# Cross-attention on one core: which engine's queue issues the first pair of block swaps

## The chip, the core and the metric

The kernel runs on one core of one Trainium2 chip. The metric is the device time of one execution in microseconds (us), the median of several runs. The engines are named as in the profile: PE is TensorE, DVE is VectorE, ACT is ScalarE, POOL is GpSimd and SP is SyncE, which only issues transfers here. "ACTq" and "SPq" are rows of an engine's instruction queue, such as the issue of a DMA transfer.

## What is computed

A layer norm, a query projection, attention of 32 heads of width 32 over a context of 256 rows, an output projection and a residual. The keys and the values are the context itself.

```python
mu, var = mean(x), var(x)                                    # x: (8, 256, 1024), float32
xn = (x - mu) * rsqrt(var + 1e-5) * ln_gamma + ln_beta
Q = split_heads(xn @ Wq.T)                                   # 32 heads of 32
K = V = split_heads(ctx)                                     # ctx: (8, 256, 1024)
scores = einsum('bhsd,bhtd->bhst', Q, K) * 32 ** -0.5        # masked where mask is False
attn = einsum('bhst,bhtd->bhsd', softmax(scores), V)
out = x + merge_heads(attn) @ Wout.T
```

## The kernel before

The order of all work is written out by hand (`manual_schedule`): each engine executes its instructions in the order in which the program lists them, and semaphores hold it where data or a buffer is not ready.

**Quads.** The work of attention is cut into N = 64 quads: eight batches, and in each eight groups of four heads (NQ = 8). One pass of the main loop (line 926) is about one quad deep on every engine. In the pass of quad n, TensorE makes the scores of quad n+1 (`scores`, L486), multiplies the probabilities of quad n-2 with the values (`values`, L629), and beside these it makes steps of the query projection of a later batch (L345, L447) and of the output projection of an earlier one (L715). The output projection and most of the query projection are Strassen-like sums of products: seven products in place of eight, whose results DVE adds out of PSUM (`take`, `store`; L753, L757) or ACT copies. The PSUM bank `po_S` or `po_A` is used again by the next product as soon as that sum has read it.

**The softmax of a quad** (`softmax_parts`) runs for n+1 during the pass of quad n. For each of four heads and two halves of 128 rows, DVE adds the mask and takes the row minimum (L522), ACT takes the exponential and its row sum (L526), DVE inverts the sums (L533, one for each head), POOL multiplies (L535, two for each head), and DVE transposes the head in 32x32 blocks (L541, `blocks`). So eight exponentials and four block transposes for each quad.

**The swaps.** After the four block transposes, half of the blocks of the tile `pT` lie on the wrong group of 32 partitions. To swap them, ACT first copies one half aside into `pc` (L547, `aside`, two copies for each quad), then two transfers of 128 KB overwrite this half with their partners (L607, the first pair, `pT<-pT`), and, after they have landed, two more bring the copies from `pc` to where the partners were (L611, the second pair, `pT<-pc`). The last block transpose, the second copy aside and the four transfers form the quad's `tail`. It runs at the end of the quad's softmax for quads 8 to 56 and for the last one, and inside the next softmax for the others. Two passes later `values` reads `pT`; `pT` has three buffers and `pc` two.

**The transfers.** All but two small ones at the start are issued by SP, in program order: for each quad the load of values (`ahead`, L144), the first pair, loads of keys, of x, of residual rows or of weights (`between`), the second pair, and in three quads of a batch also 4, 6 and 6 transfers of 64 KB that move the normalized x of a later batch between partitions (`move_x`, L332). Stores of results (L758) come from the sums in PSUM. Every transfer raises one of eight completion semaphores, given out in turn in program order; before an issue that reuses one, the issuing engine waits for the transfer that had it before.

In two quads of a batch, ACT also normalizes half of a later batch's x (`ln_norm`, L252), between the tail of one quad and the exponentials of the next.

Of the kernel before, what the change touches and what calls it, by code (L numbers as in the profile page):

```python
# [59 lines left out]
def xattn_kernel(  # L60
# [11 lines left out]
    nc = tc.nc  # L72
# [4 lines left out]
    NQ = NC  # L77
# [4 lines left out]
    K = 32  # L82
# [4 lines left out]
    N = B * NQ  # L87
# [405 lines left out]
            pass  # L493

    tails = []


    def softmax_parts(n, copies=(), ahead=(), between=(), hooks={}, fill=()):

        fill = list(fill)

        def fill_in():
            if fill:
                fill.pop(0)()

        pss = scs[n]  # L510
        pT = pTs[n] = ptp.tile([P, 2, NI, NH, NS, K], F32, tag="pT", name=f"pT_{n}")
        pc = asp.tile([P, NI, NH, NS, K], F32, tag="pc", name=f"pc_{n}")
        es, mns, dens = {}, {}, {}

        def exps(j, part=range(NS)):
            if 0 in part:
                es[j] = ep.tile([P, NS, T], F32, tag="e", name=f"e_{n}_{j}")
                mns[j] = sm.tile([P, NS], F32, tag="mn", name=f"mn_{n}_{j}")
                dens[j] = sm.tile([P, NS], F32, tag="den", name=f"den_{n}_{j}")
            e, mn, den = es[j], mns[j], dens[j]  # L520
            for s in part:
                nc.vector.tensor_tensor_reduce(  # L522
                    out=e[:, s, :], in0=pss[j][:, s, :], in1=mbs[n // NQ], scale=1.0,
                    scalar=NO_SCORE, op0=ALU.add, op1=ALU.min, accum_out=mn[:, s : s + 1],
                )
                nc.scalar.activation(  # L526
                    e[:, s, :], e[:, s, :], AF.Exp, bias=mn[:, s : s + 1], scale=-1.0,
                    accum_out=den[:, s : s + 1],
                )

        def normalize(j):
            rden = sm.tile([P, NS], F32, tag="rden", name=f"rden_{n}_{j}")
            nc.vector.reciprocal(rden, dens[j])  # L533
            for s in range(NS):
                nc.gpsimd.tensor_scalar(  # L535
                    es[j][:, s, :], es[j][:, s, :], rden[:, s : s + 1], 1.0,
                    ALU.mult, ALU.mult,
                )

        def blocks(j):  # L540
            nc.vector.transpose(  # L541
                pT[:, :, :, j, :, :].rearrange("p a i s k -> p (a i) s k"),
                es[j].rearrange("p s (b t) -> p b s t", t=K),
            )

        def aside(j):
            nc.scalar.copy(pc[:, :, ts(j, 2)], pT[:, 1, :, ts(j, 2)])  # L547

        if n == 0:
            for j in range(NH - 1):  # L550
                exps(j, (0,))
            yield
            exps(NH - 1, (0,))
            fill_in()
            yield
            for j in range(NH):
                exps(j, (1,))
            normalize(0)
            fill_in()
        else:  # L560
            exps(0)
            while tails:
                tails.pop()()
            late = "p1" in hooks
            if not late:
                for done in list(pvs):
                    copy_at(done)
            exps(1)
            for hook in hooks.get("soon", ()):
                hook()  # L570
            exps(2)
            normalize(0)
            for hook in hooks.get("p1", ()):
                hook()
            exps(3)
            if late:
                for done in list(pvs):
                    copy_at(done)
        if n <= NQ:
            for copy in copies:  # L580
                copy()
        for hook in hooks.get(0, ()):
            hook()
        normalize(1)
        fill_in()
        blocks(0)
        for hook in hooks.get(1, ()):
            hook()
        normalize(2)
        fill_in()  # L590
        blocks(1)
        aside(0)
        normalize(3)
        fill_in()
        blocks(2)
        while fill:
            fill_in()
        if n > NQ:
            for copy in copies:
                copy()  # L600

        def tail():
            blocks(3)
            aside(1)

            for r in range(2):
                nc.sync.dma_start(pT[ts(2 * r, K), 1], pT[ts(2 * r + 1, K), 0])  # L607
            for load in between:
                load()
            for r in range(2):  # L610
                nc.sync.dma_start(pT[ts(2 * r + 1, K), 0], pc[ts(2 * r, K)])  # L611

        for load in ahead:
            load()
        if n < NQ or N - NQ < n < N - 1:
            tails.append(tail)
        else:
            tail()
        yield
# [16 lines left out]
    def copy_at(n):  # L636
        b, c = divmod(n, NQ)
        k, c = divmod(c, NK)
        if c == 0:
            ats[b, k] = atp.tile([P, NK, NS, NA, K], F32, tag="at", name=f"at_{b}_{k}")  # L640
        for r, pv in enumerate(pvs.pop(n)):
            nc.scalar.copy(
                ats[b, k][:, c, :, ts(r, 2), :], pv.rearrange("p a s k -> p s a k")
            )
# [262 lines left out]
    for b in range(B - 1):  # L907
        done, ends = 0, b == B - 2
        for i, counts in enumerate(steps_of(b)):
            n = NQ * (b + 1) + i  # L910
# [227 lines left out]
```

## Time and profile before

| | |
|---|---|
| time, median of 3 runs | 577.23 us (576.55 to 578.54) |
| profiled execution, first to last instruction (span) | 577.0 us |
| PE busy | 567.3 us (98%) |
| DVE, ACT, POOL busy | 460.4, 411.7, 409.8 us |
| granted TensorE clock, mean | 0.997 |
| first-pair transfers issued by SP | 128, 3.1 us to landing (median) |

The span is the profiled execution's own time from its first to its last instruction, and no other time of that execution is given. The median of the runs is 0.23 us above it. A row of the timeline gives the start, the duration, engine, line and operation, and in brackets the idle time before it and what ended it. A row of the waits gives the engine and line that waited, for whom, the total in us, the number of times and the longest. Issues of transfers are not counted as busy time.

### The profile page before, as it was taken

Reading aid. Unit: us, or ns where it says so; the run is one execution under the profiler, and the core shown is the slowest. Engines: PE = TensorE matmul, PEld = TensorE weight load, DVE = VectorE, ACT = ScalarE, POOL = GpSimd, SP = SyncE. Lnnn points to the kernel's source line nnn. Section 1 sums busy time; section 2 is a strip of 40 time slices with the busy share of each in tenths; the row PEclk is TensorE's granted clock in tenths of the full one; section 3 lists DMA queues with packets and bytes.
Section 4 is the critical chain, followed back from the end, with each engine's and each line's share of the span. In section 5 each row is a group of like instructions: output and inputs, shape, how many; then the busy total and the mean of one; then the engine's idle time right before and its main releaser. Section 6 shows DMA issues by size and latency. Waiting matters only on the chain. (4 is left out here: it accounts for less than half of the span.)

```text
span 577.0 us, 20128 instructions
## 1 busy us (share of the span) xinstructions
PE 567.3 (98%) x7162; PEld 394.2 (68%) x7162; DVE 460.4 (80%) x1695; ACT 411.7 (71%) x1425; POOL 409.8 (71%) x677
## 2 busy tenths in 40 slices
PE   8999998999999999999999999999999999999997
PEld 8788784667667777677676677667766767755543
DVE  5888887788877879979888788988878878779823
ACT  4697886677667877688677867768767776769810
POOL 1778898889896896876568675676658657448770
PEclk9999999899999999999999999999999999999999
DMA  8974766656677777957678856687567864446751
GB/s 304 394 206 126 208 161 180 192 148 166 185 220 222 200 208 207 271 166 201 188 213 228 211 138 189 212 240 206 148 161 236 224 170 130 130 138 178 199 166 73
DMA packets 50100, 111.69 MB, mean 194 GB/s; under 512 B 9424, under 2 KB 10192, under 8 KB 50000
## 3 DMA queue, kind: packets, MB, share of 16 engines
q1 hardware_dynamic: 49712, 110.40, 66.8%
q8 instruction: 57, 0.93, 0.7%
q14 instruction: 43, 0.35, 0.2%
q10 hardware_dynamic: 288, 0.01, 0.0%
HBM read 60.04 MB, written 10.49 MB: 122 GB/s over the span
## 5 line engine op out<-in xcount | busy, mean ns | idle before, releaser
L535 POOL TENSOR_SCALAR e<-e,rden 128x256 f32<-128x256 f32 x512 | 236.0, 478 | 116.9 <-DVE rden L533 114.4
L526 ACT ACTIVATE e<-e,mn 128x256 f32<-128x256 f32 x512 | 253.9, 501 | 50.7 <-DVE mn L522 49.6
L541 DVE STREAM_TRANSPOSE pT<-e 128x512 f32<-128x512 f32 x256 | 180.9, 707 | 44.7 <-POOL e L535 32.7
L522 DVE CUSTOM_DVE_ANT_0 e<-sc,mb 128x256 f32<-128x256 f32 x512 | 185.4, 416 | 26.4 <-PE sc L486 26.0
L547 ACT COPY pc<-pT 128x512 f32<-128x512 f32 x128 | 79.0, 617 | 72.1 <-DVE pT L541 36.6
L526 ACT ACTIVATION_READ_ACCUMULATOR e<-e,mn 128x1 f32 x512 | 97.9, 191 | 0.0
L345 PE MATMUL pq<-xnT,wq 128*128 128x256 f32 (+1 forms) x368 | 84.1, 383 | 0.6 <-ACT qa L354 0.6
L345 PEld LDWEIGHTS pq<-xnT,wq 128*128 128x128 f32 x368 | 68.9, 190 | 15.4 <-issue 3.7
L629 PE MATMUL pv<-pT,v 64*32 64x128 f32 x4096 | 74.7, 274 | 3.5 <-DMA v<-in_kv_dram 2.9
L629 PEld LDWEIGHTS pv<-pT,v 64*32 64x32 f32 x4096 | 57.5, 105 | 26.7 <-issue 14.7
L486 PEld LDWEIGHTS sc<-k,qa 32*128 32x128 f32 x1024 | 46.2, 184 | 41.9 <-issue 23.6
L715 PE MATMUL po_S<-wo,at 128*128 128x512 f32 x152 | 74.3, 606 | 0.0
L486 PE MATMUL sc<-k,qa 32*128 32x256 f32 x1024 | 73.6, 401 | 0.1
L715 PE MATMUL po_A<-wo,at 128*128 128x512 f32 x128 | 61.2, 620 | 0.3 <-ACT qa L354 0.3
L715 PE MATMUL po_S<-wo,s 128*128 128x512 f32 x104 | 49.9, 606 | 0.0
L533 DVE RECIPROCAL rden<-den 128x2 f32<-128x2 f32 x256 | 37.6, 147 | 7.7 <-ACT e L526 6.8
L522 DVE DVE_READ_ACCUMULATOR2_ANT mn<- 128x1 f32 x512 | 42.5, 83 | 0.0
L715 PEld LDWEIGHTS po_A<-wo,at 128*128 128x128 f32 x128 | 23.4, 193 | 26.2 <-issue 24.5
L447 PEld LDWEIGHTS pq_A<-xnT,wq 128*128 128x128 f32 x320 | 37.3, 192 | 4.8 <-issue 3.6
L715 PEld LDWEIGHTS po_S<-wo,at 128*128 128x128 f32 x152 | 25.8, 190 | 19.7 <-issue 19.1
L447 PE MATMUL pq_A<-xnT,wq 128*128 128x128 f32 x320 | 37.3, 275 | 0.0
L748 POOL TENSOR_TENSOR r<-r,p 128x512 f32<-128x512 f32 x23 | 29.4, 1278 | 7.1 <-DMA r<-in_x_dram 3.3
(96 smaller groups left out, 608.7 us busy)
## 6 DMA issues: line engine op xcount, KB each, us to landing
v<-in_kv_dram SPq DMA_DIRECT2D x64, 256.0 KB, 3.9
pT<-pT SPq DMA_DIRECT2D x128, 128.0 KB, 3.1
pT<-pc SPq DMA_DIRECT2D x128, 128.0 KB, 3.5
ring<-kept_T SPq DMA_DIRECT2D x18, 512.0 KB, 5.2
k<-in_kv_dram SPq DMA_DIRECT2D x32, 256.0 KB, 3.1
x<-in_x_dram SPq DMA_DIRECT2D x14, 512.0 KB, 5.1
r<-in_x_dram SPq DMA_DIRECT2D x28, 256.0 KB, 5.1
out_dram<-r SPq DMA_DIRECT2D x28, 256.0 KB, 3.0
```

Source lines behind the costliest of these rows:

```text
L345: nc.tensor.matmul(pqs[n], wq[:, o, c, :], xnTs[b](c), start=(c == 0), stop=(c == NC - 1),)
L447: nc.tensor.matmul(pqs[b][:, o, :], w[:, c], x_[:, c], start=begins and o + c == 0, stop=c == NK - 1, skip_group_check=True,)
L486: nc.tensor.matmul(scs[n][j][:, s, :], qa[r, n % NQ, ts(s, P)], ks[n - n % 2][r, n % 2, :], start=True, stop=True,)
L522: nc.vector.tensor_tensor_reduce(out=e[:, s, :], in0=pss[j][:, s, :], in1=mbs[n // NQ], scale=1.0, scalar=NO_SCORE, op0=ALU.add, op1=ALU.m ...
L526: nc.scalar.activation(e[:, s, :], e[:, s, :], AF.Exp, bias=mn[:, s : s + 1], scale=-1.0, accum_out=den[:, s : s + 1],)
L533: nc.vector.reciprocal(rden, dens[j])
L535: nc.gpsimd.tensor_scalar(es[j][:, s, :], es[j][:, s, :], rden[:, s : s + 1], 1.0, ALU.mult, ALU.mult,)
L541: nc.vector.transpose(pT[:, :, :, j, :, :].rearrange("p a i s k -> p (a i) s k"), es[j].rearrange("p s (b t) -> p b s t", t=K),)
L547: nc.scalar.copy(pc[:, :, ts(j, 2)], pT[:, 1, :, ts(j, 2)])
L629: nc.tensor.matmul(pvs[n][r][j * HD : (j + 1) * HD], vs[n][ts(r, 2 * K), i, ts(j, HD)], pT[ts(r, 2 * K), :, i, j, :, :], start=(i == 0), s ...
L715: nc.tensor.matmul(po, operand(b, name)[:, c], wo[:, which, c], start=begins and c == 0, stop=c == NK - 1, skip_group_check=not begins,)
L748: nc.gpsimd.tensor_tensor(r, r, p1s[b], ALU.add)
```

## The change

For quads 10 to 56 the first pair of swaps is issued on ACT's queue, in program order right behind the quad's second copy aside, and no longer on SP's. The loads and the second pair stay on SP, in their order. 47 quads with two transfers each are 94 issues.

```diff
     tails = []
+    BY_ACT = range(NQ + 2, N - NQ + 1)
 ...
             blocks(3)
             aside(1)
 
+            queue = nc.scalar if n in BY_ACT else nc.sync
             for r in range(2):
-                nc.sync.dma_start(pT[ts(2 * r, K), 1], pT[ts(2 * r + 1, K), 0])
+                queue.dma_start(pT[ts(2 * r, K), 1], pT[ts(2 * r + 1, K), 0])
             for load in between:
                 load()
             for r in range(2):
                 nc.sync.dma_start(pT[ts(2 * r + 1, K), 0], pc[ts(2 * r, K)])
```

## The prediction

> **What bounds the kernel now.** I read the waits of PE and SP first, then the busy time of each engine batch by batch, then the timeline around the tails. Waits of PE, of ACT for DVE's minima, and of SP's queue:
>
> ```profile
> PE pv L629 <- DMA v<-in_kv_dram: 2.9, 2, 2.1
> PE pv L629 <- DMA pT<-pT: 0.5, 1, 0.5
> ACT e L526 <- DVE mn L522: 49.6, 48, 3.6
> SPq L611 <- DMA pT<-pT: 75.9, 59, 6.2
> ```
>
> SP waits long for the first pairs to land (75.9 us), but PE has waited for a swap once, for 0.5 us. Busy time of two batches, from scores to scores (the stretch and its length; busy PE, weight loads, DVE, ACT and POOL with their instructions; granted clock, busy share of the DMA engines, GB/s):
>
> ```profile
> 293.33:361.26 67.93, 67.93 (x922) 48.06 (x921) 58.21 (x213) 51.39 (x179) 45.95 (x80) 1.00 0.70 194
> 361.26:430.21 68.95, 68.10 (x921) 48.20 (x921) 58.47 (x212) 51.52 (x179) 45.99 (x80) 1.00 0.70 195
> ```
>
> In the first batch PE is busy for every one of the 67.93 us, at full clock; in the second, 0.85 us are missing. So PE sets the time, 67.93 / 8 = 8.49 us for a quad, and a change of issuing engine cannot shorten it by more than the waits that PE has inside quads 10 to 56. ACT, at 51.39 of 67.93 us, seems to have room, but it is in a loop with DVE and POOL, which has to be counted quad by quad.
>
> **What the change can save.** The 0.85 us are one late load of values:
>
> ```profile
> 357.06 1.15 SPq L607 DMA_DIRECT2D pT<-pT  x2
> 358.25 0.57 SPq L136 DMA_DIRECT2D k<-in_kv_dram  x1
> 358.87 0.43 SPq L130 DMA_DIRECT2D x<-in_x_dram  x1
> 360.45 1.15 SPq L611 DMA_DIRECT2D pT<-pc  x2
> 361.65 5.03 SPq L332 DMA_DIRECT2D xnT<-xe  x6
> 366.77 0.53 SPq L758 DMA_DIRECT2D out_dram<-r  x1
> 367.39 0.41 SPq L144 DMA_DIRECT2D v<-in_kv_dram  x1
> 367.89 1.15 SPq L607 DMA_DIRECT2D pT<-pT  x2
> ...
> 370.90 0.86 PE L629 MATMUL pv<-pT,v 64*32 64x128 f32 x36 [0.85 <-DMA v<-in_kv_dram]
> ```
>
> SP was late: it had spent 357.06 to 358.21 on quad 39's first pair, and after its loads it stood from 359.30 (358.87 + 0.43) to 360.45 for that pair's landing. With the pair on ACT, issued when the copy ends, both fall away, and the second pair, the six moves and the load of values come 1.15 + 1.15 = 2.3 us earlier. So this wait goes: -0.85 us. The other wait for values (2.9 - 0.85 = 2.05 us) is for quad 8, whose load and the swaps before it come ahead of quad 10; I leave it. No other PE wait in the range is for a transfer, so the swaps' own landing, sooner or later, is worth nothing.
>
> **What it adds on ACT.** The price of an issue on ACT at this size is not in the trace. The rows next to it are SP's issue of the same pair (quad 39's, above, and quad 46's behind its copy), and the two small issues of ACT beside four loads of SP at the start:
>
> ```profile
> 412.98 0.62 ACT L547 COPY pc<-pT 128x512 f32<-128x512 f32 x1 [1.50 <-DVE pT L541]
> 413.62 1.14 SPq L607 DMA_DIRECT2D pT<-pT  x2
> ...
> 0.72 0.41 ACTq L195 DMA_DIRECT2D gam<-in_gamma_dram  x1
> 1.16 0.45 ACTq L196 DMA_DIRECT2D bet<-in_beta_dram  x1
> 0.72 1.80 SPq L130 DMA_DIRECT2D x<-in_x_dram  x4
> ```
>
> SP issues 0.02 us after the copy's end (412.98 + 0.62 = 413.60), takes 1.15 us for the pair (357.06 to 358.21) and goes on 0.04 us later. At the start ACT's issues took 0.41 and 0.45 us where SP's took 0.45 on average (1.80 / 4), so I charge ACT what SP pays: C = 0.02 + 1.15 + 0.04 = 1.21 us from the end of a copy aside to ACT's next operation. The low end is two issues at 0.41 and 0.45, C = 0.96 with the gaps; the high end is one more SP issue of 0.57 waited for by each of ACT's, C = 1.21 + 1.14 = 2.35. No gain on ACT is possible, since nothing leaves its queue. The issue must wait for the copy's end, so nothing of it lies under the copy; what is queued behind it are the next quad's exponentials, and behind these POOL's scaling, DVE's block transposes and DVE's sums out of PSUM.
>
> Now the loop. The first and the last exponential of quad 34, and the copy aside behind it, where POOL ran without a pause:
>
> ```profile
> 302.96 0.51 ACT L526 ACTIVATE e<-e,mn 128x256 f32<-128x256 f32 x1
> 307.13 0.19 ACT L526 ACTIVATION_READ_ACCUMULATOR e<-e,mn 128x1 f32 x1
> 309.32 0.62 ACT L547 COPY pc<-pT 128x512 f32<-128x512 f32 x1 [1.01 <-DVE pT L541]
> ```
>
> Exponentials 4.36 us (302.96 to 307.32), then 2.00 us through DVE, POOL and DVE to the copy, 0.62 us for it: 6.98 us. With C this is 8.19 us, 0.30 under PE's 8.49; but two quads of each batch carry an L252 of 1.24 us right at this place. I follow one batch, quads 44 to 47 (the copy of quad 43 ends late for reasons of its own, so lateness starts at zero):
>
> ```profile
> 388.01 0.62 ACT L547 COPY pc<-pT 128x512 f32<-128x512 f32 x1
> 388.53 1.24 ACT L252 ACTIVATE x<-x,shift,rstd 128x1024 f32<-128x1024 f32 x1
> 389.68 0.49 ACT L526 ACTIVATE e<-e,mn 128x256 f32<-128x256 f32 x1
> 393.83 0.19 ACT L526 ACTIVATION_READ_ACCUMULATOR e<-e,mn 128x1 f32 x1
> 398.08 0.49 ACT L526 ACTIVATE e<-e,mn 128x256 f32<-128x256 f32 x1
> 402.23 0.19 ACT L526 ACTIVATION_READ_ACCUMULATOR e<-e,mn 128x1 f32 x1
> 406.40 0.51 ACT L526 ACTIVATE e<-e,mn 128x256 f32<-128x256 f32 x1 [0.82 <-DVE mn L522]
> 410.57 0.20 ACT L526 ACTIVATION_READ_ACCUMULATOR e<-e,mn 128x1 f32 x1
> 414.88 0.51 ACT L526 ACTIVATE e<-e,mn 128x256 f32<-128x256 f32 x1 [1.29 <-DVE mn L522]
> 415.79 0.19 ACT L526 ACTIVATION_READ_ACCUMULATOR e<-e,mn 128x1 f32 x1
> 416.43 0.16 DVE L533 RECIPROCAL rden<-den 128x2 f32<-128x2 f32 x1
> 417.18 0.69 DVE L757 TENSOR_TENSOR r<-po_S,r 128x512 f32<-128x512 f32 x1
> 419.03 1.45 PE L715 MATMUL po_S<-wo,s 128*128 128x512 f32 x3
> ```
>
> Lateness of a quad's first exponential: quad 44, 388.63 + C + 1.24 - 389.68 = C + 0.19 = 1.40. Quad 45: the last exponential of 44 ends at 394.02 + 1.40, the copy 2.62 later, then C and the second L252 (1.24): 400.49 against 398.08, 2.41 late. Quad 46: 402.42 + 2.41 + 2.62 + C = 408.66 against 406.40, 2.26. Quad 47: 410.77 + 2.26 + 2.62 + C = 416.86 against 414.88, 1.98. So the brackets of 0.82 and 1.29 us in which ACT waited for DVE are eaten, and more. In quad 47 the first reciprocal has 0.45 us to spare (the second exponential ends at 415.98, it starts at 416.43); behind it in DVE's order stands the sum that frees `po_S`, which ends at 417.87, 1.16 us before PE writes that bank again at 419.03. So PE waits 1.98 - 0.45 - 1.16 = 0.37 us. In general lateness is 4C - 2.86 and PE's wait 4C - 4.47, which begins at C = 1.12. Five batches have such a quad (15, 23, 31, 39, 47): 5 x 0.37 = 1.9 us. `po_S` is the late thing that takes over.
>
> **A second tie.** The built program's order shows all 94 issues on ACT's queue (so the change does what it says), and what they wait for besides the copy: the eight completion semaphores run through both queues, so in quads 15, 23, 31, 39, 47 and the ones after them ACT's second issue waits for the third of the six moves that SP issued just before, and the first for the second pair of the quad before. In quad 40 ACT is ready at 361.90 + 0.6 = 362.5 (361.90 is where its copy ends). By SP's rows above, the moves start at 361.65 now and 2.3 us earlier then, at 359.35; the third is out after half of 5.03 us, at 361.9, and lands 2.1 us later (rows below), so ACT is held some 1.5 us, and less where SP is less late.
>
> ```profile
> 361.28 0.62 ACT L547 COPY pc<-pT 128x512 f32<-128x512 f32 x1 [0.37 <-DVE pT L541]
> xnT<-xe SPq DMA_DIRECT2D x96, 64.0 KB, 2.1
> ```
>
> Much of it falls into the slack behind quads 40 to 43; I take 0.2 us for each of five batches, 1.0 us, with 0 and 5 x 1.5 = 7.5 as ends.
>
> **Sum.** 1.9 + 1.0 - 0.85 = +2.05 us on the span of 577.0, so 579.05, and with the 0.23 us by which the median exceeds the span, 579.3 us. About 0.3% (1.73 us) is what can be told from no change.
>
> **Rivals.** (1) Not slower: an issue on ACT costs what its two small ones did, C = 0.96. Lateness in quad 47 is then 4 x 0.96 - 2.86 = 0.98, under 0.45 + 1.16 = 1.61, PE waits for nothing and keeps the earlier load: 577.23 - 0.85 = 576.4 us. It decides below C = 1.12. For it speaks that these are ACT's only issues in the trace; against, that they carry 4 KB where SP's swaps take 0.57 against its loads' 0.45. Together with a C barely above 1.12 and no hold by the moves, 0.30 to end within 0.3%.
>
> (2) Issues of ACT and SP wait for each other. SP issues through most of a quad, so with a quarter of an SP issue of 0.57 waited for each time, C = 1.21 + 0.3 = 1.51; PE then waits 4 x 1.51 - 4.47 = 1.57 us in each of five batches, 7.9 us: 577.23 + 7.9 + 1.0 - 0.85 = 585.3 us. The start speaks against it: both engines issued at 0.72 us, and neither took twice its time. Chance 0.12. The Trainium skill, page Perfetto Trace Analysis, section DMA Instruction — HWDGE, has the descriptor generator locked for one sequencer at a time, with the wait for the lock inside the profiled issue; by that rule this rival would be the forecast, and the rows at 0.72 us do not agree with it.
>
> (3) The hold behind SP's moves is paid in full, 1.5 us in each of five batches: 577.23 + 1.9 + 7.5 - 0.85 = 585.8 us. For it: SP was six us behind the copy in quad 40 (367.89 against 361.90). Against: the pairs that made it late are gone. Chance 0.10.
>
> **How the numbers follow.** My forecast with its C between 1.19 and 1.4 has 0.43 (slower); rivals 2 and 3 have 0.22 (slower): 0.65. Within 0.3%: 0.30. Faster by over 0.3% would need 1.73 us where PE has 0.85 to give: 0.05. The range goes from just under rival 1, 576.2, to beyond rivals 2 and 3, 588.
>
> **What would show it.** Right: issue pairs of about 1.15 us on ACT behind L547; ACT's wait for DVE's minima (49.6 us) shrunk to a fraction; PE waits of some tenths for L757 or L753 at `po_S` in quads 31, 39, 47; no wait at 370. Wrong: ACT pairs under 0.9 us, or over 1.4; PE without a gap from 110 to 540 us; or PE waits in other places, such as scores or the query bank.

## The result, and the profile after

| | before | after |
|---|---|---|
| time, median of 4 runs each, side by side | 577.1 us (576.55 to 578.54) | 601.3 us (600.47 to 604.75) |
| span of the profiled execution | 577.0 us | 598.4 us |
| PE busy | 567.3 us | 573.0 us |

The changed kernel is slower by 4.2%: ratio 1.042, 95% interval 1.038 to 1.046, or 24.2 us. The forecast was 579.3 us (576.2 to 588.0), so the direction was right and the size was far off. The profiled execution of after took 600.47 us with a span of 598.4: about 2 us lie around the span. In the experiments below, one of the four executions of the kernel with shortened scalings was in a slower state (598.66 us) and is left out.

The waits of the kernel after, in the form of those shown of before (line numbers are one or two higher):

```profile
PE po_S L717 <- DVE r L759: 14.6, 13, 2.6
PE pv L631 <- DMA v<-in_kv_dram: 1.7, 1, 1.7
PE pv L631 <- DMA ring<-kept_T: 1.1, 1, 1.1
ACT e L527 <- DVE mn L523: 54.8, 43, 3.0
ACT e L527 <- DMA xnT<-xe: 10.4, 3, 4.0
SPq L613 <- DMA pT<-pT: 225.6, 73, 7.7
```

PE has a new wait, 14.6 us in 13 places, for DVE's sum that reads `po_S`. ACT's wait for DVE's minima was to shrink from 49.6 us and is 54.8. SP's wait for first pairs has grown from 75.9 to 225.6 us, but PE's waits for transfers are 2.8 us, 3.4 before, so late swaps are not the loss. The two batches of the prediction's table, again from scores to scores:

```profile
302.18:376.97 74.79, 70.44 (x921) 48.78 (x920) 59.92 (x214) 52.01 (x181) 46.06 (x81) 0.98 0.68 190
376.97:450.69 73.72, 69.35 (x921) 48.36 (x920) 58.46 (x211) 51.19 (x178) 46.07 (x80) 1.00 0.64 176
```

They were 67.93 and 68.95 us long; now PE lacks 4.4 us in each, while DVE, ACT and POOL have about as much to do as before. So the loss is waiting for the most part. (PE's own busy time is 2.5 and 1.3 us longer; 1.7 us of the first is a stretch at half clock, told of below.) Which engines it waits for is told by the chain that ended last (section 4 of the page); these are its shares by engine, before and after:

```profile
PE 34%; DVE 1%; POOL 1%; DMA 1%; ACT 0%; issue 0%; SPq 0%; DVEq 0%
```

```profile
PE 37%; POOL 18%; DVE 14%; DMA 12%; ACT 9%; issue 5%; ACTq 4%; SPq 1%; DVEq 0%; POOLq 0%
```

Before, the chain could be followed back only to 366.2 us, just ahead of the late load of values, so its shares sum to 37% of the span; over that part it runs almost on PE alone. After, it covers the whole span, and POOL, DVE and ACT hold 41% of it, ACT's issues 4%: the loop of the softmax has become a second bound. One stall of PE from quad 46 to quad 47, the place that the prediction had worked out (it shows the same rows of before):

```profile
426.20 0.51 ACT L527 ACTIVATE e<-e,mn 128x256 f32<-128x256 f32 x1 [1.29 <-DVE mn L523]
430.07 0.71 PE L486 MATMUL sc<-k,qa 32*128 32x256 f32 x8
432.78 0.62 ACT L548 COPY pc<-pT 128x512 f32<-128x512 f32 x1 [1.55 <-DVE pT L542]
433.43 1.16 ACTq L609 DMA_DIRECT2D pT<-pT  x2
434.69 0.51 ACT L527 ACTIVATE e<-e,mn 128x256 f32<-128x256 f32 x1 [1.30 <-DVE mn L523]
436.63 0.69 DVE L759 TENSOR_TENSOR r<-po_S,r 128x512 f32<-128x512 f32 x1
437.37 2.84 PE L717 MATMUL po_S<-wo,s 128*128 128x512 f32 x6 [1.30 <-DVE r L759]
437.56 2.82 POOL L536 TENSOR_SCALAR e<-e,rden 128x256 f32<-128x256 f32 x6 [0.54 <-DVE rden L534]
```

The pair takes 1.16 us on ACT, and 1.29 us pass from the copy's end (433.40) to the next exponential (434.69). From quad 46's first exponential to quad 47's are 8.49 us, 7.20 to the end of the second copy and 1.29 for the issue. PE's quad is 8.51 us. That is the finding in one line: the loop is as long as PE's quad, so lateness is not made up. Before, the same step was 7.20 of work and a wait of 1.29 for DVE's minima: the issue fills that wait. (The bracket "1.30 <-DVE mn" of after is not a wait for DVE: ACT was issuing. That is why the total for that wait did not shrink.)

One quad is not the whole of it, because two quads of a batch also carry an L252. In quads 41 to 48 of after the eight stretches from first exponential to second copy's end are 57.8 us together, eight issues with their gaps (1.29 each) are 10.3, and the L252 make the gaps of quads 43 and 44 longer by 1.1 us each: 70.3 us of loop, where PE is busy for about 68 (67.93 and 68.10 before). So each such batch adds some 2 us that PE must wait out.

Two more things cost extra: holds, in which ACT stands ahead of an issue until an earlier transfer with the same semaphore has landed, and long issues. In quad 40 ACT is held ahead of the pair, behind SP's six moves, and in quad 47 the second issue is long:

```profile
374.00 6.14 SPq L332 DMA_DIRECT2D xnT<-xe  x6
376.99 0.62 ACT L548 COPY pc<-pT 128x512 f32<-128x512 f32 x1 [0.41 <-DVE pT L542]
380.10 1.37 ACTq L609 DMA_DIRECT2D pT<-pT  x2
381.58 0.51 ACT L527 ACTIVATE e<-e,mn 128x256 f32<-128x256 f32 x1 [3.97 <-DMA xnT<-xe]
...
442.01 2.62 ACTq L609 DMA_DIRECT2D pT<-pT  x2
```

From the copy's end at 377.61 to the first issue at 380.10 are 2.49 us; the pair at 442.01 takes 2.62 us instead of 1.16. The holds of over half a us stand in quads 15, 16, 24, 31, 32 and 40 and are some 10 us together.

### The profile page after: what moved, and what is told of

Same layout as the page of the kernel before. It is cut to its first block, busy times and chain, and to the rows that moved or that the text cites. A ratio compares the mean times of both kernels' runs of the same rounds, so it can differ in the third digit from the quotient of the medians.

```text
span 598.4 us, 20014 instructions
## 1 busy us (share of the span) xinstructions
PE 573.0 (96%) x7162; PEld 394.2 (66%) x7162; DVE 466.0 (78%) x1695; ACT 412.5 (69%) x1425; POOL 410.4 (69%) x677
## 4 chain that ended last, share of the span: by engine, by line
PE 37%; POOL 18%; DVE 14%; DMA 12%; ACT 9%; issue 5%; ACTq 4%; SPq 1%; DVEq 0%; POOLq 0%
POOL e L536 15%; PE pq L345 8%; DMA pT<-pT 6%; DVE pT L542 6%; ACT e L527 5%; PE po_S L717 5%; PE sc L486 5%; PE po_A L717 4%; PE pv L631 4%; ACTq L609 4%; DVE e L523 4%; PE pq_A L447 3%; DMA x<-in_x_dram 3%; ACT pc L548 3%; PE po_end L784 2%
## 5 line engine op out<-in xcount | busy, mean ns | idle before, releaser
L527 ACT ACTIVATE e<-e,mn 128x256 f32<-128x256 f32 x512 | 253.9, 500 | 77.2 <-DVE mn L523 54.8
L534 DVE RECIPROCAL rden<-den 128x2 f32<-128x2 f32 x256 | 39.1, 153 | 56.3 <-ACT e L527 54.5
L717 PE MATMUL po_S<-wo,s 128*128 128x512 f32 x104 | 52.5, 632 | 9.3 <-DVE r L759 9.3
L717 PE MATMUL po_A<-wo,at 128*128 128x512 f32 x128 | 59.5, 605 | 1.1 <-DVE qa L463 0.9
L717 PEld LDWEIGHTS po_S<-wo,s 128*128 128x128 f32 x104 | 18.2, 193 | 28.1 <-issue 16.1
```

Source lines behind the costliest of these rows:

```text
L527: nc.scalar.activation(e[:, s, :], e[:, s, :], AF.Exp, bias=mn[:, s : s + 1], scale=-1.0, accum_out=den[:, s : s + 1],)
L717: nc.tensor.matmul(po, operand(b, name)[:, c], wo[:, which, c], start=begins and c == 0, stop=c == NK - 1, skip_group_check=not begins,)
```

## The experiments

Two theories stood at the start. A: the time that ACT spends behind the copy is in a loop with DVE and POOL, and only that time matters. B: the loss is in the holds behind SP's moves, or in the transfers and SP's queue, whatever ACT does. Ratios are to the kernel before in runs on the same chip (medians of 576.6, 574.1 and 574.7 us in the three sets); they are the recorded ones, and the quotient of two medians differs from them by up to 0.3 points (hundredths of the time before).

**ACT's time without the transfers.** Copies in place take the issue's room; every transfer stays on SP.

```diff
             blocks(3)
             aside(1)
+            if n in BY_ACT:                                # quads 10 to 56
+                nc.scalar.copy(es[3], es[3])
+                nc.scalar.copy(es[2], es[2])               # left out in the second kernel
+                nc.scalar.copy(es[1][:, 0, :], es[1][:, 0, :])
```

> The kernel before, all transfers on SP as there; behind the second copy aside of quads 10 to 56 ScalarE does three more copies in place, of tiles whose work is done (512, 512 and 256 columns): some 1.2 us of ScalarE in the place where the issues stand in the changed kernel, and nothing else of them. Theory A (the loss of 24.2 us is ScalarE's own time in the loop): most of it comes back, 594 to 602 us. Theory B (the time itself costs little, the rest is ScalarE being held behind SyncE by the shared completion semaphores and by slow issues): the formula of the prediction at C = 1.2 holds, PE waits of 0.3 to 0.8 us at po_S in quads 23, 31, 39 and 47, 578 to 582 us.

> The same with two copies more (512 and 256 columns), some 0.7 us. Below the threshold of 1.12 us that the prediction worked out. Theory A with a cost in proportion: half of the loss, 587 to 591 us. Theory B and the formula: no loss, 576.5 to 578 us.

With three copies: 588.6 us, ratio 1.020 (1.016 to 1.023). With two: 581.7 us, 1.009 (1.006 to 1.012). Each time lies between the two theories. The place of the prediction, quad 47, in the kernel with three:

```profile
425.67 0.62 ACT L547 COPY pc<-pT 128x512 f32<-128x512 f32 x1 [1.49 <-DVE pT L541]
427.54 0.51 ACT L526 ACTIVATE e<-e,mn 128x256 f32<-128x256 f32 x1
430.16 1.13 PE L719 MATMUL po_S<-wo,s 128*128 128x512 f32 x2 [1.07 <-DVE r L761]
```

1.25 us on ACT (426.29 to 427.54) make PE wait at the same place as in the changed kernel, for 1.07 us, with no issue on ACT at all. This is nearly half of the loss (1.020 of 1.042). A batch of this kernel, from quad 33's first exponential to quad 41's, takes 70.29 us (302.81 to 373.10) where it took 67.93 before: some 2 us more, as in the sum over a batch above. The kernel with two copies has next to no waits there, and its smaller loss I could not trace to one place:

```profile
PE pv L632 <- DMA v<-in_kv_dram: 3.3, 2, 1.7
PE pv L632 <- DMA pT<-pT: 1.1, 1, 1.1
PE po_S L718 <- DVE r L760: 1.0, 2, 0.6
```

**Where the holds are.** The changed kernel with the pairs of quads beside SP's moves (n % 8 in 0, 7) kept on SP, and its reverse.

```diff
-    BY_ACT = range(NQ + 2, N - NQ + 1)
+    BY_ACT = [n for n in range(NQ + 2, N - NQ + 1) if n % NQ not in (0, NQ - 1)]   # third kernel
+    BY_ACT = [n for n in range(NQ + 2, N - NQ) if n % NQ in (0, NQ - 1)]           # fourth kernel
```

> The changed kernel, but the pairs of the quads whose number leaves 7 or 0 when divided by 8 stay on SP (there ScalarE waited for moves and second pairs of SyncE's queue): 36 quads on ScalarE. Theory A: 36/47 of the loss, 594 to 597 us. Theory B: without the holds little is left, 577 to 582 us.

> The other way round: only the pairs of quads 15, 16, 23, 24, 31, 32, 39, 40, 47 and 48 are issued by ScalarE. Theory A: 10/47 of the loss, 581 to 584 us. Theory B: most of the loss, 588 to 598 us.

Not beside the moves: 598.5 us, 1.037 (1.031 to 1.042), above the range of A and far above B. Only beside them: 578.7 us, 1.004 (1.001 to 1.006), under the range of A and far under B. So the cost is not in proportion to the number of issues either. ACT's waits for transfers, third kernel and fourth:

```profile
ACT e L527 <- DMA pT<-pT: 13.3, 5, 3.4
```

```profile
ACT e L527 <- DMA pT<-pT: 6.7, 3, 2.5
ACT e L527 <- DMA xnT<-xe: 3.0, 1, 3.0
```

The third kernel has 35 pairs on ACT and the fourth 11 (quad 55 too), not 36 and 10. The holds did not go when those quads went back to SP: in the third kernel they stand in quads 17, 25, 26, 33, 41 and 49, 8.1 us in all, because the completion semaphores are given out in turn and every change of the order deals them anew. So it did not take the holds out; but 8 us of holds are not most of its loss of 21 us. In the fourth, holds of 4.4 us in quads 16, 32 and 40 and eleven issues cost some 2 us together, when the quads between them have room. Theory B in its first form falls: the holds alone are too short, and they cost little where the loop can make them up.

**Cutting the loop.** If the loop is the bound, a shorter loop must give the time back, with all issues, holds and transfers in place. My first cut took three quarters of the last heads' exponentials, the second also of POOL's scaling of them; both kernels leave out work, and only their time is of use.

```diff
+                w = T // 4 if n in BY_ACT and j > 1 else T
                 nc.scalar.activation(
-                    e[:, s, :], e[:, s, :], AF.Exp, ...
+                    e[:, s, :w], e[:, s, :w], AF.Exp, ...
 ...                                                        # ninth kernel only:
                 nc.gpsimd.tensor_scalar(
-                    es[j][:, s, :], es[j][:, s, :], rden[:, s : s + 1], 1.0,
+                    es[j][:, s, :w], es[j][:, s, :w], rden[:, s : s + 1], 1.0,
```

> The changed kernel, with four of the eight exponentials of quads 10 to 56 (the last two heads) over 64 of their 256 columns, which leaves out three quarters of those exponentials and of their sums. The pairs on ACT, their holds and their transfers stay. Theory A (the loop of ACT, DVE and POOL has become as long as PE's quad: 4.36 us of exponentials + 2.83 to the end of the second copy aside + 1.29 for the issue = 8.48 us against 8.51, so that no lateness is ever made up): four exponentials of about 0.18 instead of 0.49 us make the loop some 1.2 us shorter, 7.3 us, lateness is made up at 1.2 us a quad, PE's waits at po_S (15.3 us) go to under 2, and the time is 575 to 580 us. Theory B (the issues, their holds and the swaps' transfers cost PE time by themselves, beside SP's queue): ACT's exponentials change little of it, 590 us or more.

> The kernel of the fifth experiment (changed kernel, exponentials of the last two heads of quads 10 to 56 over 64 of 256 columns), with POOL's scaling of those two heads over the same 64 columns too; what is left out is three quarters of these exponentials and scalings. Pairs, holds and transfers stay. Theory A2 (the loop runs through POOL: from its second wait for DVE's reciprocal to the end of six scalings without a pause 2.82 us, then transpose, copy and issue; the last heads' exponentials lie beside it): the path is now 0.8 to 1.2 us shorter, about 7.4 us against PE's 8.51, lateness is made up, PE's waits at po_S fall from 12.8 to under 3 us, ratio to before 1.00 to 1.015, so 577 to 585 us. Theory B (no loop, the issues and transfers themselves cost PE's time): as the fifth, ratio 1.04, about 600 us.

The first cut: 599.4 us, 1.041 (1.035 to 1.047). Nothing came back, against theory A as I had put it. ACT's short exponentials and quad 46 in it, from first exponential to second copy:

```profile
L528 ACT ACTIVATE e<-e,mn 128x64 f32<-128x64 f32 x188 | 62.7, 338 | 0.0
```

```profile
427.81 0.51 ACT L528 ACTIVATE e<-e,mn 128x256 f32<-128x256 f32 x1 [1.29 <-DVE mn L523]
434.31 0.62 ACT L549 COPY pc<-pT 128x512 f32<-128x512 f32 x1 [1.48 <-DVE pT L543]
```

Four exponentials of 0.34 in place of 0.50 us took some 0.6 us off ACT, but the stretch is 7.12 us (427.81 to 434.93) against 7.20 in the changed kernel (426.20 to 433.40). So the path does not run through the last exponentials. It runs through POOL: from DVE's second reciprocal POOL works nearly without a pause for six scalings (2.82 us above). In the changed kernel DVE's third transpose waits for it in 46 of the 47 quads and the last one in 33; in the other 14, quad 46 among them, a sum of DVE stands ahead of the last transpose. Then come copy and issue. The second cut shows it: 587.3 us, ratio 1.022 (1.020 to 1.024). Its rows:

```profile
L538 POOL TENSOR_SCALAR e<-e,rden 128x64 f32<-128x64 f32 x188 | 57.3, 320 | 17.7 <-DVE rden L535 17.0 <-DMA ring<-kept_T 0.3
```

```profile
PE po_S L719 <- DVE r L761: 6.4, 10, 1.3
```

```profile
414.62 0.51 ACT L528 ACTIVATE e<-e,mn 128x256 f32<-128x256 f32 x1 [1.29 <-DVE mn L523]
420.87 0.62 ACT L550 COPY pc<-pT 128x512 f32<-128x512 f32 x1 [1.23 <-DVE pT L544]
```

The stretch is 6.87 us (414.62 to 421.49), 0.25 shorter than in the first cut, and the ratio falls by 1.9 points, 11.0 us of 574: 47 quads by 0.25 us are 11.8. Over quads 10 to 55 the mean stretch is 7.26 us in the changed kernel, 7.21 in the first cut and 6.92 in the second. My expectations of 577 to 585 us and of under 3 us at `po_S` were too low: I had hoped for 0.8 us off the path. A scaling of 64 columns still takes POOL 0.32 us where one of 256 takes 0.48, and DVE takes over as what ends last: its third transpose waits for POOL in only 7 of 47 quads now (47 in the first cut), and in quad 46 it starts 0.68 us after the second, right behind it, where it was 0.91. That the time follows the stretch, and not the number of issues, is what a theory of issues and transfers alone (ratio 1.04 again) cannot give.

**Every second quad.**

```diff
-    BY_ACT = range(NQ + 2, N - NQ + 1)
+    BY_ACT = range(NQ + 2, N - NQ + 1, 2)
```

> The changed kernel, with the first pair on ACT in the even quads 10 to 56 only (24 of 47). Theory A (loop): two quads take 8.48 + 7.19 = 15.7 us of loop against 17.0 of PE, 1.35 us are made up in two quads, against 2.3 us that the two L252 add in a batch of eight, and up to 2.4 us of holds in quads 16, 24, 32, 40 and 48; PE's waits at po_S under 4 us in all, time 577 to 581 us. A price for each issue, whatever stands around it: 24/47 of 24.2 us, 12.4 us, so 589 us.

Measured 581.7 us, ratio 1.012 (1.008 to 1.016). Half of the issues cost 29% of the loss, not half; the time is a little above theory A's range and far under 589. Waits of PE in it:

```profile
PE pv L631 <- DMA v<-in_kv_dram: 3.4, 2, 2.4
PE po_S L717 <- DVE r L759: 1.4, 2, 0.9
```

The waits at `po_S` are nearly gone (1.4 us). PE's waits for late loads (3.4 us) were 2.9 before, and ACT is held for 7.6 us in quads 16, 24, 32 and 40; what makes up most of the 1.2% that is left stays open.

**Holds and long issues as plain ACT time.** The first kernel's three copies, and more copies where the changed kernel was held or issued long.

```diff
+    HELD = {15: (3, 2, 1), 16: (3, 2, 1), 24: (3, 2), 32: (3, 2, 1, 1), 38: (3,), 40: (3, 2, 1, 1), 47: (3, 2), 48: (3, 2)}
 ...
                 nc.scalar.copy(es[1][:, 0, :], es[1][:, 0, :])
+            for j in HELD.get(n, ()):
+                nc.scalar.copy(es[j], es[j])
```

> The kernel before with the three copies of the first experiment (about 1.25 us of ACT in each of quads 10 to 56), and more copies behind them where ACT was held or issued long in the changed kernel: about 1.6 us in quads 15 and 16, 1.1 in 24, 2.1 in 32, 0.5 in 38, 2.1 in 40, 1.1 in 47 and 48; no transfer moves. Theory A (only ACT's time behind the copy matters; the holds and long issues are such time): PE's waits at po_S rise from 7.4 to about 15 us, time 588.6 + 6 to 9 = 594.5 to 598 us. Theory B (the rest of the changed kernel's loss comes from its transfers and SP's order): 588 to 591 us.

Measured 594.1 us, ratio 1.034 (1.030 to 1.038): 1.4 points above the three copies alone; PE's waits at `po_S` rose to 9.9 us, not to 15. So time like that of the holds and long issues costs as ACT time too, without any transfer moved.

**SP's order.** SP's six moves behind the next load of values, on the kernel before and on the changed one.

```diff
         ahead = [partial(load_v, n)] if n > 1 else []
+        if n:
+            ahead += [partial(move_x, *args) for args in moves[n - 1]]
 ...
-        for args in moves[n]:
-            move_x(*args)
```

> The kernel before with the six moves of a pass issued by SP behind the next load of values instead of ahead of it; all swaps on SP. If the two late loads of values (PE pauses of 2.05 us at 99.13 and 0.85 at 370.05, the first with 3.4 us of half clock behind it, 1.7 us) are late for SP's order: up to 4.6 us less, 572 to 575 us. If they are late for the buffer that they load into, 576 to 577 us as before.

> The changed kernel with SP's six moves behind the next load of values, as in the eighth experiment. PE's waits for values (1.70 + 0.74 + 1.07 us) go; the waits at po_S (15.3 us), which come from ACT's time in the loop, stay. 601.3 - 3.5 = 597.8 us, ratio 1.032 to 1.038. If the loss were the order of SP's queue (loads and swaps late), most of it would go: under 585 us.

On the kernel before: 572.9 us against 574.1, ratio 0.997 (0.995 to 0.998), within the time expected, with a gain of some 2 us out of the 4.6 at most, and the only version here that beats both kernels. The value load that PE had waited 2.05 us for, before and then in this kernel:

```profile
93.96 3.75 SPq L332 DMA_DIRECT2D xnT<-xe  x6
97.81 0.53 SPq L144 DMA_DIRECT2D v<-in_kv_dram  x1
```

```profile
90.93 0.53 SPq L144 DMA_DIRECT2D v<-in_kv_dram  x1
91.52 4.44 SPq L332 DMA_DIRECT2D xnT<-xe  x6
```

It is out seven microseconds earlier, and PE waits for no load of values any more. On the changed kernel: 593.9 us, 1.033 (1.030 to 1.035), one point less than without it. The waits at `po_S` stay:

```profile
PE po_S L717 <- DVE r L759: 14.7, 14, 1.9
PE po_S L717 <- DVE r L755: 2.5, 3, 1.3
```

**The account.** On 577.1 us: ACT's plain 1.25 us for each quad, 1.020, 11 us; holds and long issues, 1.034 - 1.020, 8 us; the rest up to 1.042, 5 us, is about what comes back when the loads of values go ahead of the moves (1.042 - 1.033, 5.5 us). The sum is the 24 us. But 2 us of that 5.5 come back on the kernel before too (0.997), so only some 3.5 belong to the change; with values first in both kernels the change still costs 3.6% (1.033 / 0.997). That last share of 5 us is argued from two differences with intervals of about half a point each, so it is good to some 3 us.

## Why the prediction was wrong in size

**The price of an issue** was right: C was to be 1.21 us and is 1.29 (the pair 1.16, as forecast 1.15; the rest are gaps). Rival 1 (0.96) is out, and so is rival 2: SP's issues next to ACT's changed nothing, since ACT's issues that ran beside one of SP's took 0.62 us on average (42 of them) and the others 0.65 (52); the first issues of a pair alone took 0.52 and 0.51, the second 0.73 and 0.76. By the Trainium skill, page Perfetto Trace Analysis, section DMA Instruction — HWDGE, the first should be the longer ones, for the lock on the descriptor generator is waited for inside the profiled issue; this trace does not agree. Of the 47 pairs on ACT 11 have a second issue of over 0.8 us, up to 2.08. That is not a price of ACT's: before, with SP alone issuing, 11 of the same 47 pairs had an issue of over 0.7 us, up to 1.89, and the two issues of a pair took 1.32 us on average, 1.27 on ACT. The forecast took the short pair for all; what the long ones wait for no run here settles.

**The loop was the step that failed.** I had 4.36 us of exponentials, 2.00 to the copy, 0.62 for it and C, 8.19 us in all, and so 0.30 us of slack in each quad. Measured are 7.20 + 1.29 = 8.49 us, 0.02 under PE's 8.51. C took 0.08 of the slack and the inner stretch 0.22 (7.20 for 6.98). The change did not lengthen that stretch: the prediction's own rows of quad 46 before (406.40, and the copy's end at 413.60) give 7.20 too. I had read it off quad 34, which is 6.98 us after the change as well. In quad 46 one of DVE's sums out of PSUM stands ahead of the last transpose, and in quad 34 none does; the rows after:

```profile
431.48 0.65 DVE L468 TENSOR_TENSOR qa<-pq_A,qa 128x512 f32<-128x512 f32 x1
432.05 0.69 DVE L542 STREAM_TRANSPOSE pT<-e 128x512 f32<-128x512 f32 x1
```

I had also added the loop up along ACT, where the first cut shows that ACT's last exponentials are not on the path.

**The lateness did not start at zero.** By the prediction's own figures a batch was 8 x 8.19 + 2 x 1.24 = 68.0 us of loop against PE's 67.93, so there was nothing to bring the lateness back to zero with; it is carried from one batch into the next. A quad's first scores give how far PE is behind, and its first exponential how far ACT is; quads 44 and 45 after, with quad 44's scores of before:

```profile
386.80 0.71 PE L486 MATMUL sc<-k,qa 32*128 32x256 f32 x8
```

```profile
403.38 0.93 PE L486 MATMUL sc<-k,qa 32*128 32x256 f32 x12
408.12 0.49 ACT L527 ACTIVATE e<-e,mn 128x256 f32<-128x256 f32 x1
417.85 0.49 ACT L527 ACTIVATE e<-e,mn 128x256 f32<-128x256 f32 x1
```

PE is 16.58 us behind (403.38 against 386.80) and stays so to quad 45. Quad 44's first exponential is 408.12 - 389.68 - 16.58 = 1.86 late (1.40 forecast), quad 45's 417.85 - 398.08 - 16.58 = 3.19 (2.41). By quad 47 PE is 16.88 behind (430.07 against 413.19 before), and the exponential is 434.69 - 414.88 - 16.88 = 2.93 late (1.98). Put into my last step, the wait of PE is 2.93 - 0.45 - 1.16 = 1.32 us, and 1.30 was measured. So the place, the releaser and the two spares at the end were right, and the lateness that went into them was 0.95 us too small. The formula 4C - 4.47, with its threshold at 1.12, falls with it: the three copies (C = 1.25) would give 0.53 us and gave 1.07.

**More places than five.** PE waits in all five quads named, 6.5 us in place of 1.9 (1.26, 0.43, 1.29, 2.18 and 1.30 in 15, 23, 31, 39 and 47), but the 13 waits for L759 are 14.6 us in all; the sum `L759` frees `po_S` late in other passes too, above all behind a hold or a long issue (1.58 us at 448.78, behind the long pair at 442.01).

**The second tie** (1.0 us taken, 7.5 as the end) was a real mechanism and too small a term: 2.49 us of hold in quad 40, for the moves, where 1.5 was worked out, and some 10 us of holds in six quads. Rival 3 had its size, 8 us with the long issues, but I put it beside a loop with slack that would swallow most of it, and the loop had none. The two costs are not rivals: they add up, because the loop can make up neither.

**The saving of 0.85 us** did not come: PE still waits at that load, 1.07 us. SP sent the load only at 381.67, behind six moves of 6.14 us and a store, 1.4 us earlier against PE's scores than before and not 2.3, and it took 4.9 us to land, where it took 3.3 before:

```profile
381.67 0.34 SPq L144 DMA_DIRECT2D v<-in_kv_dram  x1
382.06 0.46 SPq L414 DMA_DIRECT2D ring<-kept_T  x1
...
386.84 1.26 PE L631 MATMUL pv<-pT,v 64*32 64x128 f32 x64 [1.07 <-DMA ring<-kept_T]
```

The bracket names the load beside it, but that one landed 6.3 us after its issue, at 388.3, when PE had gone on. The load of values landed at 386.59, 0.25 us ahead of PE, the lag of before (370.66 and 370.90). So PE still waits for the load of values.

**A small one:** 0.23 us from span to time was wrong too. About 2 us lie around the span (600.47 against 598.4); the 0.23 set one execution's span against other executions' median.

## What to carry to other kernels

Before work is added to an engine that is a third idle, find the loop that it is in, add the loop's parts along the path that ends last (here POOL's, not the engine's own), and compare the sum with the bounding engine's time for the same step: the slack is that difference, not the idle share. When the slack is near zero, small delays are not made up but carried over, and holds that cost little elsewhere cost most of their length (8 us for some 11 us of copies in the seventh kernel). Take the loop over a whole batch, with every quad's own extra work in it, and not off the one quad that runs smoothest.

## What the runs showed of the hardware

- The clock fell to half for some 3.4 us behind a pause of PE of over 2 us, once in before and once in after. PE's pause of 2.18 us and the 4 us behind it, after (the granted clock is the third number from the right):

```profile
361.82:364.00 2.18, 0.01 (x1) 0.01 (x1) 1.56 (x7) 2.18 (x11) 0.93 (x2) 1.00 0.30 71
364.00:368.00 4.00, 4.00 (x6) 1.50 (x6) 3.59 (x9) 2.31 (x10) 3.77 (x7) 0.58 0.49 115
```

  In before it is the pause of 2.05 us at 99.13 (granted 0.65 from 101.18 to 106), so the late load there cost 1.7 us (half of 3.4) beyond its wait. It is no rule: behind a pause of 2.58 us at 151.46 in after, the clock stayed at 1.00.
- An issue of 128 KB on ACT takes 0.51 us as the first of a pair and 0.60 as the second (medians), like SP's before (0.51 and 0.58); its place in the loop made it dear, not its length.
- Eight completion semaphores shared in turn between two issuing queues tie them: ACT stood up to 2.49 us for transfers that it neither issued nor needs.
